# A two-layer graph network on one core: weights ahead of rows at the start, state and candidate as whole-tile operations, LeakyReLU moved to ScalarE, and new times in the planner

## The chip, the core and the metric

The kernel runs on one core of a Trainium2 chip. The core's engines each work through their own instructions in order and wait for each other by semaphores: TensorE (PE in the profile; PEld is its weight load) multiplies matrices, VectorE (DVE) does elementwise work and reductions, ScalarE (ACT) does activations and copies, GpSimd (POOL) does three tiny operations per layer norm, and SyncE (SP) issues every DMA. The metric is the device time of one execution in microseconds (us).

## The reference, cut to what matters

There are 128 graphs of 128 nodes with 256 features, all fp32. Layer 0 is a gated graph network of three steps, layer 1 is a graph attention; each has a layer norm and a ReLU in front and a residual sum behind.

```python
h = relu(layernorm(x)); A = (adj != 0)
for i in range(3):
    aggr = einsum('bst,bsd->btd', A, h @ weight[i])
    gi, gh = aggr @ w_ih.T + b_ih, h @ w_hh.T + b_hh      # split in r, z, n
    r, z = sigmoid(i_r + h_r), sigmoid(i_z + h_z)
    n = tanh(i_n + r * h_n)
    h = (1 - z) * n + z * h
x = x + h
h = relu(layernorm(x)); Wh = h @ W.T
e = leaky_relu(s1[:, :, None] + s2[:, None, :], 0.2)       # s1 = Wh @ a1, s2 = Wh @ a2
att = softmax(where(adj == 0, -inf, e))
x = x + einsum('bij,bjo->bio', att, Wh)
```

## The kernel before, in words

**Tiling.** Four graphs form a group (`G = 4`, 32 groups `g`), so a tile of features is 128 partitions by 1024 elements: two chunks of 128 features by 512 node columns. A *step* is one layer `l` of one group, 96 in all. `plan` puts them in order so that consecutive steps belong to different groups: in the middle of the run three other steps lie between two layers of one group. The last three are (31,1), (30,2), (31,2).

**One step.** `gru_step` computes the gate products with a seven-product scheme on half tiles. It runs two blocks (`blocks`), the first for reset gate and hidden candidate, the second for update gate and input candidate. Each block has seven products of mostly three matmuls each, in this order: `u` (L703), `m7` (L706), `u` again (L709), `c1[0]` (L712), `u` again (L714), `c2` (L721), `c1[1]` (L723). The bank `u` accumulates over its three products and is read between them: ScalarE copies it (L705), VectorE adds `m` to it into `c2` (L711), ScalarE copies it again (L716), VectorE adds again into `c22` (L720). TensorE can't write the third product into `u` before L711 has read it; the `c1[0]` product lies between.

Behind the products, `candidate` (L629) forms `(r+1)*v` in two operations, one for each feature half `o`. `add_half` (L780) adds the input part, `update` (L773) makes z. `state` is one task for each half: a tanh by ScalarE (L637), then three VectorE operations on 128x512 (L639, L641, L645). The second half's task to finish starts what follows: the next layer's inputs, or `epilogue`.

**Prologue and epilogue.** `prologue` normalizes a group's rows, makes the mask `A`, and transposes the rows to columns, by TensorE and ScalarE for the groups below 4 (`to_columns`, L462, L472), through DRAM by DMA for the others (`to_columns_by_blocks`). `epilogue` does the residual, the second norm and the attention. Its rows `x1` are loaded a second time (`load_x1`, L816) and added to `h` at L886; scores are formed at L903, spread by a DMA or, for the last three groups (`late`), by a TensorE transpose (L913). ScalarE adds the row score (L939, function Identity), VectorE takes `max(0.2 e, e)` (L946), masks (L952) and reduces (L958); ScalarE takes the exp (L962), `pp` is the transposed exp (L971, copied by L975), `pq` and `po` are the two products of the attention, `hs` the copy between them (L995), L1010 the final sum, then the store. The last group runs its epilogue in two parts of two graphs.

**What sets the order.** The order of every queue is written out by a planner at build time (`Order`), and the chip keeps it. Tasks yield (engine, length, time ready, room), and the planner keeps a clock for each engine: an operation starts at the later of its engine's clock and its input plus `HOP = 0.2`. `rooms` tells it when a shared buffer comes free; `fill` places elementwise work beside a product, `matmuls` places free TensorE work, `finish` runs what a step needs. The lengths are constants in the code, for example 0.62 for a 128x512 VectorE operation and `LAND = 2.5` for a DMA to land; the second load of the rows is taken as 4.0 (`LAND + 1.5`). The tile pools add the real semaphores afterwards: a wrong time in the planner gives a wait on the chip, not a wrong result.

**The start.** L92 to L133 issue the first loads from SyncE: the rows of group 0 in two DMAs, `weight[0]`, the reset part of `w_ih`, the adjacency, `w_hh` for the reset gate, the rest of `w_ih`, the rest of `w_hh`, the other weights, biases, the next groups. `given_weights` (L356) multiplies `weight[l]` into `w_ih` on TensorE, and `stationary_sums` (L321 to L339) form the weight sums of the seven-product scheme. Lines 1092 to 1099 and 1083 give the planner the times at which these are expected.

Of the kernel before, what the change touches and what calls it, by code (L numbers as in the profile page):

```python
# [14 lines left out]
P = 128  # L15
D = 256
# [11 lines left out]
def preln_gnn_kernel(  # L28
# [63 lines left out]
    xt_0 = io.tile([P, G, D], F32, tag="xt", name="xt_0", bufs=XT)  # L92
    for i in range(0, G, 2):
        dma(xt_0[:, i : i + 2, :], x[i : i + 2].rearrange("b t d -> t b d"))
    xts, ats = {0: (xt_0, (2.7, 3.7))}, {}
# [18 lines left out]
    ats[0] = load_adjacency(0), 6.4  # L114
    load_gates(whh, w_hh_t, slice(0, 1))
    load_gates(wih, w_ih_t, slice(1, 3))
# [54 lines left out]
    class Order:  # L171
        def __init__(self):
            self.free = dict.fromkeys((PE, ACT, DVE, POOL, SP, "port"), 0.0)
            self.tasks = []

            self.rooms = {"misc": [0.0] * 3, "tq": [0.0] * 2, "h": [0.0] * ROWS, "x1": [0.0] * 2, "prT": [0.0] * 2}
            self.next, self.room_of = dict.fromkeys(self.rooms, 0), {}
# [22 lines left out]
        def open(self, room, name):  # L200
# [6 lines left out]
            if room == "prT":  # L207
                return work.tile([P, G, P], F32, tag="prT", name=name)
# [220 lines left out]
    def norm_apply(src, graphs, rstd, nb, ready, name, h=None):  # L429

        for k in graphs:
            t = yield (ACT, 0.5, ready, "h") if h is None else (ACT, 0.5, ready)
            if h is None:
                h = order.open("h", f"h_{name}")
# [189 lines left out]

    def candidate(s, r, v, ready):

        for o in (1, 0):
            s.v_ready[o] = yield DVE2, 0.62, ready[o]
            put(nc.vector.scalar_tensor_tensor(  # L629
                v[:, o, :], r[:, o, :], 1.0, v[:, o, :], ALU.add, ALU.mult  # L630
            ))

    def state(s, o, old, new, v, z, ready):
# [4 lines left out]
        t = yield DVE2, 0.62, t  # L638
        put(nc.vector.tensor_tensor(new[:, o, :], old[:, o, :], n, ALU.subtract))  # L639
        t = yield DVE2, 0.62, t - HOP  # L640
        put(nc.vector.scalar_tensor_tensor(  # L641
            new[:, o, :], z[:, o, :], 1.0, new[:, o, :], ALU.add, ALU.mult
        ))
        t = yield DVE2, 0.62, t - HOP
        put(nc.vector.scalar_tensor_tensor(new[:, o, :], new[:, o, :], 0.5, n, ALU.mult, ALU.add))  # L645
        s.halves.append(t)
        if len(s.halves) == C:
            s.hT, s.aT = new, None
# [13 lines left out]
    def gru_step(s, last):  # L662
# [97 lines left out]
        s.v_ready = [0.0, 0.0]  # L760
        half_task = order.add(0, candidate(s, r, v, (banks["c1_1"], t1)))
# [395 lines left out]
```

## Time and profile before

| | |
|---|---|
| median of 3 runs | 2144.81 us (2143.91 to 2145.84) |
| the profiled execution, its own time | 2144.55 us |
| its span, first to last instruction | 2142.7 us |
| TensorE busy, matmuls | 2118.7 us (99%), 10779 records |
| VectorE busy | 1782.2 us (83%) |
| ScalarE busy | 1295.0 us (60%) |
| GpSimd busy | 119.1 us (6%) |
| mean granted TensorE clock | 0.997 |

A row of a timeline gives the start and the length in us, the engine, the line of the kernel, the operation and its tiles, and in brackets how long the engine sat idle before it and what ended that. A row of the waits names who waited for whom, the sum in us, the number of times, and the longest. A row of the groups gives the shape, the count, the busy time and the mean of one in ns. An fp32 matmul of the program leaves two records. A window's row gives the busy time of PE, PEld, DVE, ACT and POOL with the number of instructions, then the granted clock, the DMA share and the GB/s.

### The profile page before, as it was taken

The numbers are of one execution on the slowest core, as the hardware profiler recorded it, in microseconds if no ns is written. First come the engines' busy times: TensorE is split into PE (matmuls) and PEld (weight loads), VectorE is DVE, ScalarE is ACT, GpSimd is POOL, SyncE is SP. The second block draws the span as 40 slices with busy tenths as digits, with TensorE's granted clock in tenths as the row PEclk, the third lists the DMA queues.
The fourth block names the chain that finished last, engine by engine and source line by source line (L and its number), as shares of the span: only waits on it lengthen the run. The fifth ranks groups of instructions, "written<-read, shape, count | busy, mean of one in ns | idle before, by whom it ended". The sixth has DMA issues, their size and how long they took to land.

```text
span 2142.7 us, 32496 instructions
## 1 busy us (share of the span) xinstructions
PE 2118.7 (99%) x10779; PEld 1882.7 (88%) x10779; DVE 1782.2 (83%) x4176; ACT 1295.0 (60%) x2859; POOL 119.1 (6%) x204
## 2 busy tenths in 40 slices
PE   8999999999999999999999999999999999999997
PEld 7888888888888888888888888888888888888886
DVE  7778888888888888888888888888888888888776
ACT  5556656565566666656655565656656566565664
POOL 1000000000000000000000000000000000000000
PEclk9999999999999999999999999999999999999998
DMA  4144353535454255553535545354542544443301
GB/s 138 39 90 89 75 122 84 124 68 130 109 117 115 59 125 109 119 113 73 125 84 127 120 88 124 70 127 105 119 113 64 120 109 109 95 90 82 84 25 40
DMA packets 659240, 209.85 MB, mean 98 GB/s; under 512 B 569856, under 2 KB 636160, under 8 KB 659072
## 3 DMA queue, kind: packets, MB, share of 16 engines
q1 hardware_dynamic: 659072, 207.77, 43.3%
q8 instruction: 85, 1.39, 0.3%
q14 instruction: 83, 0.68, 0.1%
HBM read 120.86 MB, written 86.83 MB: 97 GB/s over the span
## 4 chain that ended last, share of the span: by engine, by line
PE 97%; DVE 2%; DMA 1%; issue 0%; SPq 0%; ACT 0%; DVEq 0%
PE c L685 34%; PE u L685 34%; PE m L685 11%; PE pa L593 8%; PE po L1003 5%; PE pq L593 3%; PE pw L356 1%; DMA x<-in_x 0%; PE pt_a L462 0%; DMA wih<-in_w_ih_t 0%; DVE prT L903 0%; DVE hT L639 0%; DMA out<-x 0%; DVE hT L641 0%; DVE c L711 0%
## 5 line engine op out<-in xcount | busy, mean ns | idle before, releaser
L773 ACT ACTIVATE z<-c,brz 128x256 f32<-128x256 f32 x384 | 185.1, 482 | 303.5 <-PE c L685 139.2
L685 PE MATMUL u<-t_h,s_hh 128*128 128x256 f32 x1152 | 343.0, 379 | 3.8 <-DVE c L711 3.8
L685 PE MATMUL c<-aT,s_f 128*128 128x256 f32 x1152 | 311.3, 379 | 0.0
L685 PE MATMUL u<-t_a,s_f 128*128 128x256 f32 x1152 | 311.3, 379 | 0.0
L738 ACT ACTIVATE r<-c,brz 128x256 f32<-128x256 f32 x384 | 174.3, 477 | 218.3 <-PE c L685 113.8
L780 DVE TENSOR_TENSOR v<-v,c 128x256 f32<-128x256 f32 x384 | 155.1, 418 | 132.1 <-ACT z L773 72.3
L685 PEld LDWEIGHTS u<-t_h,s_hh 128*128 128x128 f32 x1152 | 218.1, 190 | 34.7 <-DVE c L711 5.0
L685 PEld LDWEIGHTS u<-t_a,s_f 128*128 128x128 f32 x1152 | 218.9, 190 | 29.8
L685 PEld LDWEIGHTS c<-aT,s_f 128*128 128x128 f32 x1152 | 218.9, 190 | 29.8
L685 PE MATMUL c<-hT,s_hh 128*128 128x256 f32 x768 | 228.5, 379 | 0.0
L716 ACT COPY c<-u 128x512 f32<-128x512 f32 x192 | 109.5, 570 | 143.2 <-PE u L685 142.5
L711 DVE TENSOR_TENSOR c<-u,m 128x512 f32<-128x512 f32 x192 | 134.2, 699 | 72.4 <-PE u L685 70.4
L708 ACT COPY m<-m 128x512 f32<-128x512 f32 x192 | 112.6, 586 | 101.7 <-PE m L685 99.3
L745 ACT ACTIVATE v<-c,bhn 128x256 f32<-128x256 f32 x384 | 173.1, 481 | 0.0
L720 DVE TENSOR_TENSOR c<-u,m 128x512 f32<-128x512 f32 x192 | 131.5, 685 | 49.2 <-ACT c L716 49.2
L685 PE MATMUL m<-t_h,s_hh 128*128 128x256 f32 x576 | 171.5, 379 | 0.0
L685 PE MATMUL c<-t_h,s_hh 128*128 128x256 f32 x576 | 171.3, 379 | 0.0
L685 PEld LDWEIGHTS c<-hT,s_hh 128*128 128x128 f32 x768 | 144.8, 190 | 19.1
L685 PE MATMUL c<-t_a,s_f 128*128 128x256 f32 x576 | 155.7, 379 | 0.0
L685 PE MATMUL m<-t_a,s_f 128*128 128x256 f32 x576 | 155.6, 379 | 0.0
L685 PE MATMUL u<-aT,s_f 128*128 128x256 f32 x576 | 155.6, 379 | 0.0
L629 DVE SCALAR_TENSOR_TENSOR v<-r,v 128x512 f32<-128x512 f32 x192 | 123.4, 684 | 30.3 <-ACT v L745 28.8
(126 smaller groups left out, 3971.5 us busy)
## 6 DMA issues: line engine op xcount, KB each, us to landing
z<-tq SPq DMA_DIRECT2D x248, 128.0 KB
h<-z SPq DMA_DIRECT2D x248, 128.0 KB
xt<-in_x SPq DMA_DIRECT2D x31, 512.0 KB
z_b<-tq_b SPq DMA_DIRECT2D x116, 128.0 KB
h_b<-z_b SPq DMA_DIRECT2D x116, 128.0 KB
x<-in_x SPq DMA_DIRECT2D x29, 512.0 KB
out<-x SPq DMA_DIRECT2D x29, 512.0 KB
z_a<-tq_a SPq DMA_DIRECT2D x112, 128.0 KB
```

Source lines behind the costliest of these rows:

```text
L593: put(nc.tensor.matmul(pa[:, k * P : (k + 1) * P], h[:, k, c * P : (c + 1) * P], A[:, k, :], start=True, stop=True,))
L629: put(nc.vector.scalar_tensor_tensor(v[:, o, :], r[:, o, :], 1.0, v[:, o, :], ALU.add, ALU.mult))
L685: put(nc.tensor.matmul(to(q), S[0][:, gate_no, weight, :], moving, start=first and q == 0 and i == 0, stop=(i == len(ends) - 1), skip_grou ...
L708: put(nc.scalar.copy(m, m7))
L711: put(nc.vector.tensor_tensor(c2, u, m, ALU.add))
L716: put(nc.scalar.copy(c1[1], u))
L720: put(nc.vector.tensor_tensor(c22, u, m, ALU.add))
L738: put(nc.scalar.activation(r[:, o, cols], src, AF.Tanh, bias=brz[:, o : o + 1], scale=0.5))
L745: put(nc.scalar.activation(v[:, o, cols], src, AF.Identity, bias=bhn[:, o : o + 1], scale=0.5))
L773: put(nc.scalar.activation(z[:, o, cols], src, AF.Tanh, bias=brz[:, C + o : C + o + 1], scale=0.5))
L780: put(nc.vector.tensor_tensor(v[:, o, cols], v[:, o, cols], src, ALU.add))
L1003: put(nc.tensor.matmul(po[:, j, :], hs[:, c, k * P : (k + 1) * P], gwt[:, c, :], start=(c == 0), stop=(c == C - 1),))
```

## The change

Five things change. (1) At the start `weight[0]` and the reset part of `w_ih` are issued ahead of the rows of group 0, and the rest of `w_ih` ahead of the adjacency and of `w_hh`; the planner's times for these follow. (2) `candidate` is one operation on 128x1024 in place of two on 128x512; `state` keeps its two tanh operations, and its three VectorE operations are done once on 128x1024, after both. (3) L946 goes; the ScalarE pass at L939 uses Prelu with alpha 0.2 in place of Identity. (4) The planner takes 5.0 for the second load of the rows (4.0 before), 4.5 for the store that frees their buffer (2.5 before), and keeps rooms for `e` and `hs`. (5) Groups 2 and 3 are transposed through DRAM too. For the last two groups `e`, `hs` and the normalized rows get other buffers, one each for both parts of the last group.

```diff
-    xt_0 = io.tile([P, G, D], F32, tag="xt", name="xt_0", bufs=XT)
-    for i in range(0, G, 2):
-        dma(xt_0[:, i : i + 2, :], x[i : i + 2].rearrange("b t d -> t b d"))
-    xts, ats = {0: (xt_0, (2.7, 3.7))}, {}
...
     load_weight(0, gate, [P, 2, H], "m")
     load_gates(wih, w_ih_t, slice(0, 1))
-    ats[0] = load_adjacency(0), 6.4
+    xt_0 = io.tile([P, G, D], F32, tag="xt", name="xt_0", bufs=XT)
+    for i in range(0, G, 2):
+        dma(xt_0[:, i : i + 2, :], x[i : i + 2].rearrange("b t d -> t b d"))
+    xts, ats = {0: (xt_0, (4.8, 5.8))}, {}
+    load_gates(wih, w_ih_t, slice(1, 3))
+    ats[0] = load_adjacency(0), 8.6
     load_gates(whh, w_hh_t, slice(0, 1))
-    load_gates(wih, w_ih_t, slice(1, 3))
...
-            self.rooms = {"misc": [0.0] * 3, "tq": [0.0] * 2, "h": [0.0] * ROWS, "x1": [0.0] * 2, "prT": [0.0] * 2}
+            self.rooms = {room: [0.0] * 2 for room in ("tq", "x1", "prT", "e", "hs")}
+            self.rooms |= {"misc": [0.0] * 3, "h": [0.0] * ROWS}
...
     def candidate(s, r, v, ready):
-        for o in (1, 0):
-            s.v_ready[o] = yield DVE2, 0.62, ready[o]
-            put(nc.vector.scalar_tensor_tensor(
-                v[:, o, :], r[:, o, :], 1.0, v[:, o, :], ALU.add, ALU.mult
-            ))
+        t = s.v_ready = yield DVE2, 1.22, ready
+        put(nc.vector.scalar_tensor_tensor(flat(v), flat(r), 1.0, flat(v), ALU.add, ALU.mult))
...
         put(nc.scalar.activation(n, n, AF.Tanh, bias=bih[:, 2 * C + o : 2 * C + o + 1], scale=1.0))
-        t = yield DVE2, 0.62, t
-        put(nc.vector.tensor_tensor(new[:, o, :], old[:, o, :], n, ALU.subtract))
-        t = yield DVE2, 0.62, t - HOP
-        put(nc.vector.scalar_tensor_tensor(
-            new[:, o, :], z[:, o, :], 1.0, new[:, o, :], ALU.add, ALU.mult
-        ))
-        t = yield DVE2, 0.62, t - HOP
-        put(nc.vector.scalar_tensor_tensor(new[:, o, :], new[:, o, :], 0.5, n, ALU.mult, ALU.add))
         s.halves.append(t)
         if len(s.halves) == C:
+            n, new_, z_ = flat(v), flat(new), flat(z)
+            t = yield DVE2, 1.22, max(s.halves)
+            put(nc.vector.tensor_tensor(new_, flat(old), n, ALU.subtract))
+            t = yield DVE2, 1.22, t - HOP
+            put(nc.vector.scalar_tensor_tensor(new_, z_, 1.0, new_, ALU.add, ALU.mult))
+            t = yield DVE2, 1.22, t - HOP
+            put(nc.vector.scalar_tensor_tensor(new_, new_, 0.5, n, ALU.mult, ALU.add))
...
-        s.x1_ready = LAND + 1.5 + (yield SP, 0.45, 0.0, "x1")
+        s.x1_ready = 5.0 + (yield SP, 0.45, 0.0, "x1")
...
-        transposed = to_columns if g < 4 else to_columns_by_blocks
+        transposed = to_columns if g < 2 else to_columns_by_blocks
...
+    def place_of_e(g):
+        if g < NG - 2:
+            return order.open("e", f"e_{g}")
+        return work.tile([P, 4, H], F32, tag="th", name=f"e_{g}")[:, 0:2, :].rearrange(
+            "p n t -> p (n t)"
+        ).rearrange("p (k s) -> p k s", s=P)
...
             put(nc.scalar.activation(
-                e[:, k, :], src, AF.Identity, bias=one[:, k : k + 1], scale=1.0
+                e[:, k, :], src, AF.Prelu, bias=one[:, k : k + 1], scale=1.0, alpha=ALPHA
             ))
...
-        t = yield DVE2, row_t, t
-        put(nc.vector.scalar_tensor_tensor(le, le, ALPHA, le, ALU.mult, ALU.max))
...
-            order.close(f"x1_{g}", t + LAND)
+            order.close(f"x1_{g}", t + 4.5)
...
-    order.take(PE, 2.8, 2.2)
+    order.take(PE, 1.5, 1.0)
...
-        order.add(1, given_weights(0, wf_0, [(reset, 5.4)])),
-        order.add(1, given_weights(0, wf_0, [(others, 9.2)])),
+        order.add(1, given_weights(0, wf_0, [(reset, 4.4)])),
+        order.add(1, given_weights(0, wf_0, [(others, 8.0)])),
...
-        order.add(1, hidden_weights(((0, 7.3), (2, 10.1), (1, 11.1)))), order.add(2, biases(17.0))
+        order.add(1, hidden_weights(((0, 9.2), (2, 10.4), (1, 11.2)))), order.add(2, biases(17.0))
```

The lines of the profile before are those of the kernel before. In the changed kernel the numbers shift by 1 to 31 (L711 becomes L716, L886 becomes L903, L939 becomes L958).

## The prediction

> **What bounds the kernel now.** I read the page first, then the waits of TensorE, then the timelines of the three places where it stands idle. The page's head:
>
> ```profile
> span 2142.7 us, 32496 instructions
> PE 2118.7 (99%) x10779; PEld 1882.7 (88%) x10779; DVE 1782.2 (83%) x4176; ACT 1295.0 (60%) x2859; POOL 119.1 (6%) x204
> PE 97%; DVE 2%; DMA 1%; issue 0%; SPq 0%; ACT 0%; DVEq 0%
> ```
>
> TensorE is busy for 99% of the span and makes 97% of the chain that ended last. Work taken from VectorE is worth something only where TensorE waits. All its waits:
>
> ```profile
> PE ps L913 <- DVE prT L903: 5.6, 1, 5.6
> PE pw L356 <- DMA wih<-in_w_ih_t: 3.9, 1, 3.9
> PE u L685 <- DVE c L711: 3.8, 3, 2.5
> PE pq L593 <- ACT prT L975: 3.3, 3, 2.2
> PE po L1003 <- DVE xt L1010: 1.5, 1, 1.5
> ```
>
> The second is the start, the third lies in the middle (0.3 at 23.7 us, 2.5 near 1820, 1.0 near 1870), the others lie in the tail. The timeline at the 2.5 us wait and at the two ends:
>
> ```profile
> 6.55 3.75 PE L356 MATMUL pw<-wih,wt 128*128 128x256 f32 x8 [3.91 <-DMA wih<-in_w_ih_t]
> 32.46 1.04 PE L462 MATMUL pt_a<-ident,h_a 128*128 128x128 f32 x8
> 1812.42 1.26 SPq L60 DMA_DIRECT2D x<-in_x  x1
> 1817.31 1.29 DVE L886 TENSOR_TENSOR x<-x,h_b 128x512 f32<-128x512 f32 x2 [2.81 <-DMA x<-in_x]
> 1821.17 0.69 DVE L711 TENSOR_TENSOR c<-u,m 128x512 f32<-128x512 f32 x1
> 2107.46 0.69 DVE L645 SCALAR_TENSOR_TENSOR hT<-hT,v 128x512 f32<-128x512 f32 x1
> 2117.61 0.69 DVE L946 SCALAR_TENSOR_TENSOR e<-e 128x512 f32<-128x512 f32 x1
> 2119.76 1.09 ACT L435 ACTIVATE h_b<-xt,norm_b 128x256 f32<-128x256 f32 x2 [2.35 <-POOL norm_b L426]
> 2122.96 0.58 ACT L975 COPY prT<-pp 128x512 f32<-128x512 f32 x1 [0.31 <-PE pp L971]
> 2134.93 0.37 ACT L975 COPY prT<-pp 128x256 f32<-128x256 f32 x1 [2.66 <-PE pp L971]
> 2138.58 0.88 DVE L1010 SCALAR_TENSOR_TENSOR xt<-po,soft,xt 128x256 f32<-128x256 f32 x2 [2.72 <-PE po L1003]
> ```
>
> In the middle rows VectorE sits 2.81 us before L886, whose rows the planner took as landed. Everything behind it, L711 too, is late, and TensorE with it. The last recurrence matmul ends at 2103.61; call that T. The tail from T to the end of the span is 39.1 us, a chain over VectorE, ScalarE and TensorE.
>
> The sum is made against the profiled execution, 2144.55 us: the span and 1.85 around it. It stands 0.26 below the median of the runs.
>
> **The start: -1.3.** The reset part of `w_ih` moves from places four and five to places two and three of SyncE's queue; the two DMAs of rows move behind it, the rest of `w_ih` (two DMAs) ahead of the adjacency and two of `w_hh`. SyncE's slots are 0.5 us apart (0.72, 1.22, 1.72). The first rows, issued at 0.72, had landed by 3.49, so 2.77 is the quickest landing here; the last DMA of the reset part, issued at 2.70, landed at 6.41, so 3.71 with a megabyte ahead of it. Issued at 1.72, it lands between 4.49 and 5.43, and TensorE starts 1.0 to 1.9 earlier than at 6.55. I take 1.3, below the middle, because the rows follow at once and share the engines. The rows land up to 2 us later. In the new order TensorE does all four weight products of layer 0 (1.7 more than before) ahead of the first transposes, and this hides them: rows landed at 6.4 at the latest, plus 3.8 from there to the end of the second half's norm as before (4.78 to 8.57), plus 1 behind the copy that now stands first in ScalarE's queue, is 11.4, when TensorE is still in those products. Without this cover the rows would cost up to 1 us. The adjacency is three slots later (1.5 us); the mask is needed only by `pa`, after the transposes.
>
> **TensorE's work: -1.7, and -0.4 moved.** Two groups lose eight transposes each. The eight at 32.46 push the next product to 33.33: 0.87 a group, 1.73. The last four `pp` transposes of group 29 stood before T and now stand after it: 0.43 out of T into the tail. The two groups add 8 stores and 8 loads of 128 KB to SyncE and four VectorE transposes of 0.69; both lie under steps 2 and 3 places off (21.9 us a step), which cover a round trip of some 10 us. Without that cover the step would wait for it.
>
> **The waits at 1820 and 1870: -3.5, and +0.5 for what is late next.** The load issued at 1812.42 had its rows at 1817.31, 4.9 later; the one at 1860.05 at 1864.29, 4.2 later; the planner took 4.0 and now takes 5.0. The store ahead of the second had been issued at 1856.34, 3.7 before the load could go; 2.5 becomes 4.5. Both waits (2.5 and 1.0) should go. What is pushed back is the epilogue, which nothing on TensorE's path waits for. Next in line is L711 late for another reason: between nothing and the 3.8 of before, I take 0.5.
>
> **State and candidate as whole tiles: nothing in the middle.** The groups by shape:
>
> ```profile
> L780 DVE TENSOR_TENSOR v<-v,c 128x256 f32<-128x256 f32 x384 | 155.1, 418 | 132.1 <-ACT z L773 72.3 <-PE c L685 56.1
> L641 DVE SCALAR_TENSOR_TENSOR hT<-z,hT 128x512 f32<-128x512 f32 x192 | 132.0, 688 | 3.4
> L946 DVE SCALAR_TENSOR_TENSOR e<-e 128x512 f32<-128x512 f32 x31 | 20.6, 665 | 0.0
> ```
>
> From 418 to 688 ns is 270 for 256 columns, so 128x1024 costs about 1.22, against 1.37 for two halves: 0.15 saved, four times in 96 steps, 58 us of VectorE. L946 saves 21.5 more. VectorE falls from 1782 to about 1705 us, all of it under TensorE. The new wait is on both tanhs: the new state is ready up to 1.5 us later than with halves. Behind the waiting operation stand the epilogue's operations and the next L711. Three steps of 21.9 us lie between two layers of a group, so nobody on TensorE's path waits; at the last step there is no such cover, which the tail counts.
>
> **Prelu for Identity: nothing by itself.** The pass was there already (402 ns for 128x128 in 116 of them); both programs load one activation table. The trace has no Prelu: bounds are 0 and, for a pass as dear as the exp at L962 with its read (397 + 191 ns), 0.2 each, 24 us of a ScalarE that is 60% busy. I take 0, since the nearest row has the same shape and operands. The Trainium skill, page "ScalarE: Activation LUTs", section "Rules for kernel authors", speaks against it: relu and max belong on VectorE, not ScalarE. By that rule keeping L946 would be right, and the sum would get back its 0.7 and the 0.43 of the last group's halves in the tail; but here ScalarE reads the tile in any case, and VectorE is the fuller engine.
>
> **The tail: -5.1.** I follow the new order of the queues with the durations of these rows. T+0.4 last `add_half`; both tanhs now stand behind the last z, T+0.9 to T+2.2; meanwhile VectorE does four of group 30's score operations (1.8), which before stood behind the state. Three operations of 1.25: state at T+6.0 (before 2108.16, T+4.55), 1.45 worse. ScalarE's exps of group 29 come behind the tanhs, to T+3.75; `pp`, copy and `pq` (1.78) end at T+6.4, transposes of the state at T+6.8. VectorE has the other scores at T+8.1, the residual 0.7, the norm's statistics 1.3, POOL 1.56: first h_b at T+11.65. The mask and reduction of group 30 now stand before the second half of group 31's norm, and end at T+12.7; before, at 2120.09, T+16.5. Its exps, `pp` and copy follow at T+15.1 (before 2122.96, T+19.35). The second norm of group 31 starts its h_b at T+19.0 to 19.8 (POOL took 1.56 and 2.36 in the two cases shown) and ends at X = T+20.1 to 20.9. From there VectorE has 7.5 us of scores, sums, mask and reductions with one exp pair and the transposes: last `prT` copy at X+5.55. Before, 7.77 lay between that copy (2134.93) and the end. The span ends at T+33.4 to T+34.2; I take 34.0, 5.1 less than 39.1. Bounds: 33 (nothing else waits) and 39 (the clock, below).
>
> **Sum.** 1.3 + 1.7 + 0.4 + 3.5 - 0.5 + 5.1 = 11.5, so 2133.0 for the profiled execution and 2133.3 against the median.
>
> **Rivals.** *A cold tail, 2136.3.* The granted clock of TensorE fell to half in the half microsecond of this row:
>
> ```profile
> 2114.40 0.60 PE L913 MATMUL ps<-ident,s 128*128 128x128 f32 x4
> ...
> 2117.50:2118.00 0.50, 0.00 (x0) 0.00 (x0) 0.45 (x2) 0.00 (x0) 0.29 (x1) 0.63 0.52 186
> ```
>
> That is 2.6 us after the last matmul had ended, and the next `pq` took 3.78 for 1.78; a gap of 2.16 at T did nothing. The new order has gaps of some 2.6 (T to the first `pp`) and 2.1. By the row the first is a toss-up; a cold `pq` and `po` cost 1 to 4, I take 3. The skill's page "TensorE: Matmul & The Clock Gate", section "Why this matters for your kernels", puts the limit at gaps of about 3 us: by it the tail stays warm, and the sum is unchanged.
>
> *The loads stay late, 2136.8.* If the landing spreads beyond 5.0, the waits of 3.5 stay or move. 4.9 is close to 5.0; but 56 of the 58 L886 had no such wait even with 4.0.
>
> *A whole-tile operation in front of L711, the other side.* TensorE's `c1[0]` product lasts 1.29 and L711 with its hops 0.7, so L711 may be 0.6 late. VectorE keeps order: a 1.22 operation begun a little late holds it. In the new order 40 of the 192 L711 have such an operation directly ahead. Above about 19 lost waits of 0.6 (11.5 us) the change is no gain; all 40 would give 2157. Against it: 84 of 192 have a 0.69 operation directly ahead now, and none but the three shown lost anything; row durations summed over the VectorE instructions between L720 and the next L711 leave at least 1.2 us in every block, as before.
>
> *The rows at the start are late, 2135.* The cover above fails and 1 to 2 come back.
>
> **How the numbers follow.** Likeliest 0.45 (2131 to 2136); cold tail 0.22; loads 0.12; whole-tile stalls 0.13, of which some 0.08 beyond the gain; start 0.08. The range 2130.5 to 2142 takes in the first three, the start and the milder stalls. The three runs spread over 0.09%, so 0.2% (4.3 us) tells a change from none. Faster, below 2140.5: 0.85; within 0.2%: 0.05; slower: 0.10.
>
> **What would show it.** Right: the first `pw` near 5.3; no wait of PE for L716 (L711's new place) near any L903 (L886's) with a DMA behind it; 5428 program matmuls; the new L647 to L651 near 1.22; one table load; T near 2097; first `pp` of the tail at half or full clock settles the cold rival. Wrong: many PE waits on L716 behind L636 or L647 to L651, or a tail of 39.

## The result and the profile after

The changed kernel takes 2141.05 us, median of 7 runs (2135.69 to 2142.27), where the kernel before, run beside it, takes 2144.81 (2143.91 to 2145.84). The ratio is 0.9976, 95% interval 0.9966 to 0.9985: it is faster, but by 3.8 us where 11.5 were forecast. Its profiled execution took 2138.47 us, 2.6 less than the median, and most of what follows is about that spread.

The head of its page, then TensorE's waits (who waited for whom, the sum in us, how often, the longest):

```profile
span 2136.7 us, 32121 instructions
...
PE 2119.0 (99%) x10763; PEld 1879.0 (88%) x10763; DVE 1724.6 (81%) x3763; ACT 1302.4 (61%) x2855; POOL 105.9 (5%) x204
...
PE 96%; DMA 1%; ACT 1%; DVE 1%; SPq 1%; issue 0%; POOL 0%; DVEq 0%; ACTq 0%; POOLq 0%
```

```profile
PE pp L988 <- ACT e L979: 4.3, 3, 2.7
PE pq L598 <- DMA e<-z_e: 3.0, 4, 1.8
PE pq L598 <- ACT prT L992: 2.3, 4, 0.7
PE pw L357 <- DMA wih<-in_w_ih_t: 1.6, 2, 1.2
...
PE u L690 <- DVE c L716: 0.3, 1, 0.3
```

What was to go went: the wait for the first weights is 1.6 instead of 3.9, and of the 3.8 on L711 (now L716) only the 0.3 of the start is left. New is the second row. It lies in the middle of the run: the product `pq` of the attention waits for `e`, which comes back transposed through DRAM (stores `z_e<-prT`, loads `e<-z_e`). The first and third rows belong to the tail.

To see the middle and the tail apart I use two numbers for every run. T is the end of the last recurrence matmul, the tail is the span behind it. The *time lost before T* is T minus TensorE's work up to there, taken from the order of its instructions at the spacing of undisturbed rows (0.431 us for 256 columns, 0.2225 for 128, 0.108 for a transpose). It holds the start, every wait, and slow matmuls. "Low clock" is the length of the tail, in half microseconds while matmuls were still to come, in which the granted clock was below full. Each ratio is to the kernel before as timed beside that run.

| run | median us (runs) | ratio to before, 95% | T | lost before T | tail | low clock in the tail |
|---|---|---|---|---|---|---|
| before | 2144.81 (7) | | 2103.60 | 15.7 | 39.1 | 10.5 |
| after | 2141.05 (7) | 0.9976 (0.9966 to 0.9985) | 2101.29 | 15.6 | 35.4 | 4 |
| e5, after again | 2140.65 (10) | 0.9975 (0.9966 to 0.9985) | 2104.84 | 19.1 | 35.5 | 4 |
| e13, after again | 2142.02 (11) | 0.9982 (0.9973 to 0.9991) | 2104.88 | 19.2 | 38.8 | 7 and 7.5 |
| e17, after again | 2142.22 (10) | 0.9982 (0.9973 to 0.9991) | 2105.84 | 20.1 | 35.3 | 4 |
| e1, ten idle products | 2139.71 (5) | 0.9968 (0.9955 to 0.9981) | 2103.66 | 17.9 | 35.5 | 4 |
| e2, planner: `e` later | 2166.70 (4) | 1.0094 (1.0079 to 1.0109) | 2126.68 | 41.0 | 38.0 | 7 and 3.5 |
| e3, halves | 2139.00 (5) | 0.9963 (0.9950 to 0.9976) | 2102.75 | 11.4 | 34.7 | 17.5 |
| e4, before + two times | 2140.66 (10) | 0.9976 (0.9966 to 0.9986) | 2098.42 | 10.5 | 39.7 | 4 and 7 |
| e6, `e` by POOL | 2148.74 (10) | 1.0011 (1.0002 to 1.0021) | 2108.12 | 22.4 | 36.2 | 7.5 |
| e7, before + start | 2144.82 (10) | 0.9999 (0.9990 to 1.0008) | 2103.26 | 15.4 | 39.3 | 4 and 7.5 |
| e8, halves, filled | 2140.54 (10) | 0.9971 (0.9962 to 0.9980) | 2105.67 | 12.5 | 34.0 | 4 and 4 |
| e9, rows by POOL | 2136.97 (5) | 0.9962 (0.9949 to 0.9975) | 2099.21 | 13.5 | 36.0 | 7.5 |
| e10, whole tiles, order of e3 | 2193.70 (4) | 1.0222 (1.0207 to 1.0237) | 2157.58 | 66.2 | 34.5 | 7.5 and 7.5 |
| e11, before + Prelu | 2145.11 (10) | 0.9997 (0.9988 to 1.0007) | 2104.56 | 16.7 | 38.6 | 11 |
| e12, e10 filled | 2194.49 (4) | 1.0224 (1.0207 to 1.0241) | 2158.11 | 66.7 | 34.6 | 14.5 |
| e14, e9 again | 2136.99 (5) | 0.9962 (0.9949 to 0.9974) | 2098.27 | 12.5 | 37.5 | 7 and 4 |
| e15, e9, first gap filled | 2136.55 (4) | 0.9960 (0.9946 to 0.9973) | 2098.23 | 12.5 | 36.7 | 7.5 |
| e16, e9, both gaps filled | 2134.35 (5) | 0.9948 (0.9935 to 0.9962) | 2098.15 | 12.4 | 34.4 | 0 |

T fell by 2.3 in the first profile. 2.16 of it is work taken out or moved behind T, as counted in the forecast. The time lost before T is the same as before although the start gained 1.8 and the old waits of 3.5 are gone: some 5 us came in somewhere. Here is the longest place, from the timeline of the changed kernel (start, length, engine, line, operation, tiles, and in brackets the idle time before; only the rows that bear on it, and of the four stores `z<-tq` the last three):

```profile
371.87 2.69 SPq L60 DMA_DIRECT2D z<-tq  x3
...
376.65 0.70 DVE L571 STREAM_TRANSPOSE prT<-e 128x512 f32<-128x512 f32 x1
378.14 3.12 SPq L60 DMA_DIRECT2D h<-z  x4
381.31 2.79 SPq L60 DMA_DIRECT2D z_e<-prT  x4
384.16 0.61 SPq L60 DMA_DIRECT2D x<-in_x  x1
385.78 1.71 SPq L60 DMA_DIRECT2D e<-z_e  x4
389.66 2.02 PE L598 MATMUL pq<-e,h_b 128*128 128x128 f32 x16 [1.81 <-DMA e<-z_e]
```

VectorE has `prT` ready at 377.35. The stores of `z_e` could go then, but in SyncE's order the loads `h<-z` of another group stand in front of them, and these wait until their own stores (the last issued by 374.56) have landed, at 378.14: 3.6 us, where the planner's `LAND` is 2.5. So the stores of `z_e` begin 3.96 us late, the loads of `e` end 10.1 us after the transpose, and `pq`, which the order puts 10.34 us behind the transpose, waits 1.81. Followed back, the chain that ended last in this stretch goes from `pq` over the landings of `e` and `z_e` to SyncE's issuing of `h<-z` at 378.

In the kernel before, the stores of `z_e` began 0.02 to 0.08 us after the transpose in all 24 groups up to 1800 us. In the new order every third group has `h<-z` in between: in the eight from 377 to 1747 us the stores began 1.4 to 4.0 us late, while in the other two of three they start at 0.02 to 0.04. That is where two runs of one program part: the first profile and e5 keep their distance within 0.1 us for some 200 us at a time, and it changes at such a `pq` (by 0.2 at 388 us, 0.4 at 585, 0.8 at 781, -0.5 at 975, -0.2 at 1367, 0.8 at 1563, 0.7 at 1758). One more change, 0.8, lies at 1824, where L716 waits 0.7 in e5. How long each trip takes varies; the place hardly does.

### The profile page after: what moved, and what is told of

The parts are those of the page before. It is cut to its first block, busy times and chain, and to the rows that moved or that the text cites. A ratio compares the mean times of both kernels' runs of the same rounds, so it can differ in the third digit from the quotient of the medians.

```text
span 2136.7 us, 32121 instructions
## 1 busy us (share of the span) xinstructions
PE 2119.0 (99%) x10763; PEld 1879.0 (88%) x10763; DVE 1724.6 (81%) x3763; ACT 1302.4 (61%) x2855; POOL 105.9 (5%) x204
## 4 chain that ended last, share of the span: by engine, by line
PE 96%; DMA 1%; ACT 1%; DVE 1%; SPq 1%; issue 0%; POOL 0%; DVEq 0%; ACTq 0%; POOLq 0%
PE c L690 34%; PE u L690 34%; PE m L690 11%; PE pa L598 8%; PE po L1027 5%; PE pq L598 3%; PE pw L357 1%; SPq L60 1%; DMA e<-z_e 1%; DMA z_e<-prT 0%; ACT e L979 0%; DMA wih<-in_w_ih_t 0%; ACT v L642 0%; PE pr_o L489 0%; DVE v L785 0%
## 5 line engine op out<-in xcount | busy, mean ns | idle before, releaser
L716 DVE TENSOR_TENSOR c<-u,m 128x512 f32<-128x512 f32 x192 | 134.0, 698 | 144.9 <-PE u L690 144.7
L721 ACT COPY c<-u 128x512 f32<-128x512 f32 x192 | 109.4, 570 | 117.3 <-PE u L690 116.9
L725 DVE TENSOR_TENSOR c<-u,m 128x512 f32<-128x512 f32 x192 | 132.0, 687 | 37.5 <-ACT c L721 36.0
L710 ACT COPY c<-u 128x512 f32<-128x512 f32 x192 | 109.5, 570 | 53.3 <-PE u L690 53.3
```

What stands on the lines that cost most here:

```text
L710: put(nc.scalar.copy(c1[0], u))
L716: put(nc.vector.tensor_tensor(c2, u, m, ALU.add))
L721: put(nc.scalar.copy(c1[1], u))
L725: put(nc.vector.tensor_tensor(c22, u, m, ALU.add))
```

## Experiments

Where a kernel has products of the identity by itself on TensorE (called idle products below), they only keep it busy, and nobody reads their result.

**e1: ten idle products in front of each `pp` of the tail.**

```diff
+            if g < NG - 1:
+                for _ in range(10):
+                    put(nc.tensor.matmul(m7[:, 0, 0:P], ident, ident, start=True, stop=True))
             for k in graphs:
                 put(nc.tensor.transpose(pp[...], e[:, k, :], ident))
```

> Changed kernel, plus ten 128x128 matmuls of the identity into the idle bank m7 in front of the transposed exps (pp) of groups 29 and 30, where TensorE has nothing to do; the order of all else is kept, and no output changes. Theory A (the spread of 2135.7 to 2142.3 of the changed kernel is a cold TensorE clock in the tail): no window of the tail is below full clock, the first pq of the tail takes about 1.8 in place of 3.6, the tail from the last recurrence matmul to the end is about 34 in place of 35.4, the runs agree within 2 us and the median falls to 2135 to 2137. Rival B (the spread comes from DMA waits in the middle): spread and median stay, 2138 to 2142.

The times lie closer (2137.88 to 2140.94), but the tail is 35.5, as in after. The clock fell all the same, at T+5.5, though no idle stretch of TensorE there was longer than 0.7 us: ahead of it TensorE had been busy for 2.2 of 3.5 us. So one long gap isn't what it takes. T came 2.4 later than in after with the same order up to there: the middle varies from run to run.

**e2: the planner is told that `e` lands 2.5 us later.**

```diff
-        return (yield from by_way_of_dram(
+        return 2.5 + (yield from by_way_of_dram(
```

> Changed kernel; the planner is told that the transposed attention e lands 2.5 us later than it took, and nothing else. Theory A (TensorE waits in the middle because pq is placed before e can have come back through DRAM): the waits of PE on e<-z_e, 5.1 us on TensorE's weight loads in the changed kernel, fall below 1, and the last recurrence matmul ends near 2096 to 2097 in place of 2101.3; median 2136 to 2138. Rival B (the whole-tile operations or the queue as a whole are late, so that waits only move): the sum of PE's waits between 50 us and the tail stays 3 or more, the time 2140 to 2142.

A miss, and an instructive one. The new time made another order, in which `pq` still waits and more waits come in:

```profile
PE u L690 <- DVE c L716: 15.1, 9, 2.8
...
PE pq L598 <- DMA e<-z_e: 3.9, 4, 1.9
```

Their cause is the same kind of trip: in this order VectorE stands in front of L458 for the features that come transposed through DRAM (`hT_a<-z_a`, 19.7 us in 9 waits, 3.5 at most), and L716 behind it is late. Here one corrected time put another trip where it is short; e4 below shows that it can also go well. The waits cost more than their own length: behind five of them (1.9 to 2.8 us each) the granted clock stood at 0.50 for 3.41 us in the middle of the run, first at 388.92, which happened in no other trace before T.

**e3: after, planned and written with state and candidate in halves as before.**

```diff
-        t = yield DVE2, 1.22, max(s.halves)
-        put(nc.vector.tensor_tensor(new_, flat(old), n, ALU.subtract))
+        t = yield DVE2, 0.62, t
+        put(nc.vector.tensor_tensor(new[:, o, :], old[:, o, :], n, ALU.subtract))
 ...
```

> Changed kernel with candidate and state on halves of 128x512 as before; start, Prelu, planner times and transposes stay as changed. Theory A (the waits on e<-z_e come from the planner's DMA times): 2 to 6 us of DMA waits of PE stay, time within 3 us of the changed kernel (2138 to 2144). Rival B (the whole-tile operations make e late): no PE wait on e<-z_e, last recurrence matmul near 2096.5. In the tail the state is ready near T+4.6 in place of T+6.0.

```profile
PE pr_o L489 <- DVE hT L653: 6.0, 1, 6.0
PE pp L991 <- ACT e L982: 4.0, 1, 4.0
...
PE pa L598 <- DMA h<-z: 0.6, 1, 0.6
```

No wait on `e` is left, and 11.4 us are lost before T. Here, up to 1940 us, `pq` stands 11.63 us behind the transpose in every group, and the stores of `z_e` begin 1.0 to 2.6 us after it, so the trip fits. Planning with the whole-tile times thus brought in the order that is short in every third group.

**e4: before, with only the two times for the second load of the rows.**

```diff
-        s.x1_ready = LAND + 1.5 + (yield SP, 0.45, 0.0, "x1")
+        s.x1_ready = 5.0 + (yield SP, 0.45, 0.0, "x1")
...
-            order.close(f"x1_{g}", t + LAND)
+            order.close(f"x1_{g}", t + 4.5)
```

> Kernel before, with only the planner's two times changed: 5.0 for the second load of the rows, 4.5 for the store that frees their buffer. Theory A (those two times remove the waits on L711 behind L886 and bring others only by chance): no wait of PE on L711 in the middle (3.5 before), time 2141 if nothing takes their place. Rival B (longer times push the epilogue into SyncE's queue and make other DMAs late, as in the changed kernel): PE waits on e<-z_e of 2 or more appear, time 2142 to 2146.

The waits at 1820 and 1870 are gone (0.3 on L711 is left, at the start) and nothing came in their place: by its progress against the profile of before it gains 2.8 near 1820 us and 1.3 more near 1870. These two constants alone make a kernel as fast as the whole change (0.9976 for both). Up to 1750 us it already lies 1.18 ahead, with a start that isn't changed at all; see the last section.

**e7: before, with only the new start.**

```diff
     load_gates(wih, w_ih_t, slice(0, 1))
-    ats[0] = load_adjacency(0), 6.4
+    xt_0 = io.tile([P, G, D], F32, tag="xt", name="xt_0", bufs=XT)
+    ...
+    load_gates(wih, w_ih_t, slice(1, 3))
+    ats[0] = load_adjacency(0), 8.6
...
-    order.take(PE, 2.8, 2.2)
+    order.take(PE, 1.5, 1.0)
```

> The kernel before with only the new order of the first loads and the planner's start times. My sum of the start said 1.3 us; the profile of the changed kernel shows 1.8. If it is 1.8 by itself, T falls from 2103.6 to about 2101.8, or as far as 2100.5 if the start runs at the full clock throughout, the waits at 1820 and 1870 stay within 1 us of 3.5 and the time is 1 to 2.5 us below the kernel before. Rival: the rows that now land later hold the first transposes, and the time is that of the kernel before within 0.5.

From 400 to 1750 us it runs 1.24 ahead of the profile of before, near the 1.3 of the forecast; but e4, with the old start, ran 1.18 ahead, so this profile alone shows nothing (see the last sections). Then the waits at 1820 and 1870 take 4.5 instead of 3.5. In the times (0.9999) it can't be told from before.

**e5: the changed kernel once more.** No edit.

> The changed kernel once more, unaltered, profiled on another occasion. If the waits in the middle belong to the written order, the waits of TensorE on e<-z_e stand at the same places with the same sizes (1.8 near 388 us, 5.1 in all in the weight loads' row), lost time before T is 15.6 as before, and the time is 2141 within 1 us. If they depend on how long each transfer through DRAM happens to take, the sum moves by 1 to 3 us between the two profiles (lost time before T 13 to 18) and the tail stays at 35.4 within 0.5.

T is 3.55 later with the same order, by the steps told above; the tail is 35.5. The waits on `e` are 5.0 in 7.

**e6: the trip of `e` issued by POOL.**

```diff
-            G, t, f"{name}_e",
+            G, t, f"{name}_e", queue=nc.gpsimd,
```

> The changed kernel with the order of PE, DVE and ACT untouched; only the eight transfers that bring the attention tile e through DRAM are issued by POOL instead of SyncE. Theory A (SyncE issues in order, and the trip of e stands behind transfers that are held for another tile's landing): the waits of TensorE on e<-z_e fall from 5.1 to under 1, lost time before T from 15.6 to 11 or 12, the time by about 4 us to 2136 or 2137. Theory B (the trip itself is too long for its place in the order, whoever issues it): the waits stay above half of 5.1 and the time stays at 2140 to 2142. A cost that could spoil it: POOL is held behind a landing, its norms come late, and TensorE then waits on h_b instead.

Worse: 2148.74. The stores now begin 0.3 to 0.5 us after the transpose (once 1.6), but the loads of `e` go only 6.4 to 8.2 us after it in every third group, and the waits are 6.6. For transfers that POOL issues the trace also has the landings, and they say why: in all 29 groups the loads begin 0.66 to 0.74 us after the last of the four stores has landed. In the eight groups in question, where SyncE issues `h<-z` from 0.4 us before the transpose to 1.8 us behind it, that store lands 2.9 to 4.7 us after its issue has ended, in most others 1.6. So in this run the trip is too long though nothing holds it in its queue: next to other transfers the stores land late. The hold in SyncE can't be the whole cause.

**e9: the loads that bring rows back (`h<-z`) issued by POOL instead, the trip of `e` left on SyncE.** The order of PE, DVE and ACT is that of after.

```diff
-            tmp.rearrange("p i g c f -> p (i g c) f"), place, C * G, t, name, "h"
+            tmp.rearrange("p i g c f -> p (i g c) f"), place, C * G, t, name, "h", nc.gpsimd,
```

> The changed kernel with the order of PE, DVE and ACT untouched; only the four loads that bring a tile of rows h back from DRAM (h<-z) are issued by POOL instead of SyncE, so that they hold nobody on SyncE while they wait for their stores to land. In every third group of the changed kernel the stores of z_e began 1.4 to 4.1 us after prT was transposed, and pq comes 10.34 us behind that transpose. Theory A (SyncE's order): these stores begin within 0.5 us, the loads of e within 5 us, the waits of TensorE on e<-z_e fall from 5 to under 0.5, lost time before T falls to 11 to 13, the time to 2136 to 2138. Theory C (the transfers share the 16 DMA engines, so whatever stands next to them slows them): the loads of e still go 6 us or more after the transpose, the waits stay above 3 and the time at 2140 or more. A cost that could hide A: rows that land later hold the products pa.

The same place as above, in its timeline:

```profile
376.36 0.70 DVE L571 STREAM_TRANSPOSE prT<-e 128x512 f32<-128x512 f32 x1
377.07 1.93 POOL L60 DMA_DIRECT2D h<-z  x4 [5.17 <-PE u L690]
377.09 4.01 SPq L60 DMA_DIRECT2D z_e<-prT  x4
381.20 0.57 SPq L60 DMA_DIRECT2D x<-in_x  x1
383.79 1.73 SPq L60 DMA_DIRECT2D e<-z_e  x4
387.40 1.95 PE L598 MATMUL pq<-e,h_b 128*128 128x128 f32 x16
```

The stores begin 0.03 us after the transpose, and `pq` follows at 10.34 without a wait. In all groups up to 1822 us the stores begin within 0.04. Two waits are left (2.0 in all, at 583 and 780), and the loads of `e` still go 5 to 7.3 us after the transpose where 4.3 is the quickest: the other expectation, that the transfers also slow each other, holds for a part, as in e6. The Trainium skill, page "Trainium Kernel Development and Optimization", section "Key Constraints", says that issuing from several engines saves only the sequencer's issue time, since all share the same 16 DMA engines; here it also took a held instruction out of the way, and the move was worth 5 us (e13 and e14 below). How much of that is the hold, and how much the way in which the transfers then fall beside each other, these runs don't part.

**e13 and e14: after and e9 once more, side by side.** No new edit.

> The changed kernel, timed beside e14 on the same chip. If the waits on e in the middle differ from run to run, as between its two profiles (T 3.55 apart with one order), its profile again shows a lost time before T somewhere between 15 and 20, the tail at 35.4 within 0.3, and the times spread over 4 us or more around 2141.

> e9 once more, against the changed kernel on the same chip. If SyncE's order is where most of the missing gain went, e14 is faster than e13 by 2.5 to 5 us in the median, and in the profile the stores of z_e begin within 0.1 us of the transpose in all groups up to 1800 us, with 1 to 3 us of waits on e<-z_e left. If e9's gain was the luck of its runs, the two agree within 1 us.

2142.02 against 2136.99, 5.0 us apart (intervals 0.9973 to 0.9991 and 0.9949 to 0.9974, which touch but hardly overlap). In the profiles the time lost before T is 19.2 against 12.5, 6.6 us by T, of which the waits on `e` show 4.4 (5.8 against 1.4). The starts of the two agree within 0.1 us, so the difference lies in the middle. The tail of e13 is 38.8, for 35.4 in the first profile with the same order. Its timeline:

```profile
2109.87 3.79 PE L598 MATMUL pq<-prT,h_b 128*128 128x128 f32 x16 [0.68 <-ACT prT L992]
...
2122.21 3.78 PE L598 MATMUL pq<-prT,h_b 128*128 128x128 f32 x16 [0.68 <-ACT prT L992]
...
2126.21 4.71 PE L1027 MATMUL po<-gwt,hs 128*128 128x256 f32 x16
```

Both `pq` ran at half clock; in the first profile of after only the first did (3.60, then 2.05).

**e15 and e16: e9 with the idle stretches of the tail filled,** in e15 in front of the first `pq` alone, in e16 of both.

```diff
+            fill = NG - 3 <= g < NG - 1          # e15: g == NG - 3
+            warm((10 if g == NG - 3 else 7) * fill)
             for k in graphs:
                 put(nc.tensor.transpose(pp[:, k * P : (k + 1) * P], e[:, k, :], ident))
+                warm(fill)
+            warm(2 * fill)
```

> e9 with products of the identity by itself on TensorE, read by nobody, that fill the idle stretches from T to the first pq of the tail: 10 ahead of the first pp, one behind each of its four transposes, 2 ahead of pq. It asks what the cold clock costs the tail, and whether the clock falls only where TensorE has little to do over some microseconds. If both hold, the granted clock stays at 1.0 up to that pq, which takes 1.8 instead of 3.6 us, and the tail falls from the 35.4 to 36.0 of the changed kernel and e9 to 34.0 to 34.6, near the 34.0 of my sum for a warm tail. If the clock falls all the same, or the tail stays at 35.4 or above with a warm clock, the rest of the tail's shortfall lies with VectorE and ScalarE.

> e15 with the same filling of the second idle stretch of the tail as well (7 products of the identity ahead of the second group's pp, one behind each of its transposes, 2 ahead of its pq). In e15 the first pq took 2.05 us instead of 3.6, but the clock fell at T+13.5, the second pq took 3.79 and the two po behind it 4.12, and the tail was 36.7. If the clock now stays at 1.0 over both, the second pq takes about 1.9, its po 3.6, and the tail falls by 2 to 3 us to 33.7 to 34.7, the forecast's 34.0 for a warm tail; the time by as much, to 2134 or 2135. If the tail stays at 36 or more with a warm clock, VectorE and ScalarE set it and the clock does not.

In e15 the first `pq` took 2.05, but the clock fell at T+13.5 and the second took 3.79: tail 36.7. In e16 the clock never fell. From its list of cores (span and mean clock) and its timeline:

```profile
core 0: 2132.6 us, clock 1.000
```

```profile
2102.99 2.05 PE L598 MATMUL pq<-prT,h_b 128*128 128x128 f32 x16
...
2113.77 2.05 PE L598 MATMUL pq<-prT,h_b 128*128 128x128 f32 x16
...
2115.87 3.91 PE L1035 MATMUL po<-gwt,hs 128*128 128x256 f32 x16
```

The tail is 34.4, the time 2134.35 (2133.84 to 2134.71), ratio 0.9948 (0.9935 to 0.9962). The kernel is the change with the loads `h<-z` on another queue and 29 products that nobody reads, and it is 7.9 us faster than the change itself beside it (e17). How much of that the products bring is less sure: the intervals of e9 and e16 overlap, but the tail is 1.5 to 3 us shorter.

**e17: after beside e16.** No edit.

> The changed kernel on the same chip for the comparison with e16: 2140 to 2142.5, with a tail of 35.4 where only one stretch of the tail is at the low clock and near 38.8 where two are, as in e13.

2142.22, tail 35.3 with one stretch at the low clock.

**e8: e3 with idle products in the last gaps.**

```diff
+            if g == NG - 1 and pairs[0] == 0:
+                warm(16)
             banks, ready = yield from to_rows(s.hT, ready, f"{name}_o", pairs)
...
+            if g < NG - 1:
+                warm(8)
             for k in graphs:
                 put(nc.tensor.transpose(pp[...], e[:, k, :], ident))
```

> The changed kernel with the state and the candidate in halves as before (as in e3), and on TensorE 16 products of the identity by itself ahead of the last state's transposes and 8 ahead of the first pp, which only keep TensorE busy (their results are read by nobody). In e3 the clock was at half from T+3 to T+20 and pr_o, pp, pq and po took 1.9, 1.6, 3.8 and 2.4 us, which is 4.5 more than at full clock. If the cold clock is on the path of the tail, the tail falls from 34.7 to between 30.5 and 32.5 and the time to 2135 to 2137 in e3's conditions. If the tail is bound by VectorE and ScalarE, it stays at 34 or more.

The tail fell by 0.7 where 2 to 4 were expected, though the low clock fell from 17.5 to 8 us; 8 of the products came to stand in front of T (1.8 us at 0.2225 each). In this order the gaps are long (6.0 and 4.0 in e3), which suggests that the low clock lies partly beside VectorE's chain; no run shows it.

**e10: whole-tile operations without their order.** The order of e3 on PE, ACT and SyncE, each whole-tile operation at the place of the second half.

```diff
         t = yield DVE2, 0.62, t
-        put(nc.vector.tensor_tensor(new[:, o, :], old[:, o, :], n, ALU.subtract))
+        if second(0):
+            put(nc.vector.tensor_tensor(flat(new), flat(old), flat(v), ALU.subtract))
+        else:
+            put(nc.vector.tensor_tensor(new[:, o, 0:1], old[:, o, 0:1], n[:, 0:1], ALU.subtract))
 ...
```

> The order of e3 (the changed kernel planned with halves) kept on PE, ACT and SyncE, but the state's three operations and the candidate's are issued over the whole tile, each at the place of the second half; the first half leaves one subtraction of a single column. It parts the whole-tile operations from the order that the planner makes with them. Theory: by themselves they cost nothing and take 55 to 60 us from VectorE; TensorE has no wait in the middle on the rows c or e<-z_e (under 0.7 in all besides the start), T lies within 1.2 of e3 (the start varies by that), and the time at 2138 to 2140. Rival (the whole-tile operation holds VectorE in front of L716): TensorE waits on c for 2 us or more in the middle and the time is above 2141.

The rival came true. Waits of TensorE, and one of the places in the timeline:

```profile
PE u L701 <- DVE c L736: 14.0, 54, 0.4
...
PE u L701 <- DVE c L727: 4.2, 9, 0.5
```

```profile
711.50 1.22 DVE L656 SCALAR_TENSOR_TENSOR hT<-z,hT 128x1024 f32<-128x1024 f32 x1
711.82 0.57 ACT L732 COPY c<-u 128x512 f32<-128x512 f32 x1 [0.40 <-PE u L701]
...
712.75 1.23 DVE L661 SCALAR_TENSOR_TENSOR hT<-hT,v 128x1024 f32<-128x1024 f32 x1
...
713.89 0.69 DVE L736 TENSOR_TENSOR c<-u,m 128x512 f32<-128x512 f32 x1
...
714.63 0.70 PE L701 MATMUL u<-hT,s_hh 128*128 128x256 f32 x2 [0.26 <-DVE c L736]
```

L736 (L725 of after) could start at 712.4, when ScalarE's copy ends, but two operations of 1.2 us stand ahead, and it starts at 713.89. The product between covers 1.29 of it. 63 such waits show as 18.2 us, and T is 54.8 later than in e3: the rest stands in rows that count as busy (PE 2150.0 for 2118.1). 54 of the 63 are at L736, the second of the two reads of the bank, where the rival had named the first. So the whole-tile operation costs nothing only in an order that was made with its 1.22; put into another, it costs some 0.9 a wait.

**e12: e10 with 16 idle products behind T.**

```diff
+            if g == NG - 1 and pairs[0] == 0:
+                warm(16)
             banks, ready = yield from to_rows(s.hT, ready, f"{name}_o", pairs)
```

> e10 with 16 products of the identity by itself on TensorE right behind T, ahead of the last state's transposes, which only keep TensorE busy. In e8 these and 16 others gave 0.7 off the tail and cost 1.8 ahead of T; here none stands ahead of T. Expected: T as in e10, the tail 0.5 to 1 shorter than e10's, the time 0.5 to 1 below e10's. If VectorE's and ScalarE's chain alone sets the tail, it is as long as e10's within 0.3.

The tail stayed (34.6 for 34.5): filling one gap alone did nothing here. The low clock began at T+6.9 instead of T+2.7, and there was as much of it.

**e11: before, Prelu for Identity and no L946, order kept.**

```diff
-                e[:, k, :], src, AF.Identity, bias=one[:, k : k + 1], scale=1.0
+                e[:, k, :], src, AF.Prelu, bias=one[:, k : k + 1], scale=1.0, alpha=ALPHA
...
-        put(nc.vector.scalar_tensor_tensor(le, le, ALPHA, le, ALU.mult, ALU.max))
```

> The kernel before with its order kept; Prelu takes the place of Identity, and L946, VectorE's maximum, is left out. By my sum nothing changes up to T, since VectorE only loses 20.6 us under TensorE (the L711 waits of 3.5 may move by 1), and the tail loses between 0.7 and 1.1: 2144 to 2146. If a Prelu is dearer than Identity (402 ns), by as much as 0.2, the tail of 39.1 gains nothing. Prelu's own duration settles it.

Prelu takes as long as Identity. The group of this pass in e11, 116 of 128x128 (the last number is the mean in ns; in before 402):

```profile
L939 ACT ACTIVATE e<-e,s 128x128 f32<-128x128 f32 x116 | 37.7, 403 | 0.3 <-DMA e<-line 0.3
```

The tail is 0.5 shorter, T 1.0 later (0.4 of it at the start, the rest behind 1000 us), and the time can't be told from before.

## Why the forecast was half right

**The start, -1.3: held in the mean.** It is 1.77 in the profile of after, where the third `u` product starts at 22.81 instead of 23.72 with one weight product of 0.86 more behind it. A single profile can't show it, since e4 gained 1.1 and e11 lost 0.3 with the old start. But at 30 us the sixteen profiles with the new start are 0.6 to 2.3 ahead of that of before, 1.35 ahead of the mean of the three with the old one. The rows of group 0 held nobody: the first transposes come right behind the weight products.

**TensorE's work, -1.73 and -0.43: held** by the count, 2.16 out of T.

**The waits at 1820 and 1870, -3.5: held** (0.6 or 0.7 came back at 1824 in e5, e13 and e17), and e4 shows that the two times do it alone. **"And +0.5 for what is late next": this step failed.** The forecast looked for it at L711, between nothing and 3.8, and said of the epilogue that nothing on TensorE's path waits for it. `pq` does. Between the runs of the new start without held trips (11.4 to 13.5 lost before T) and the four profiles of after (15.6, 19.1, 19.2, 20.1) lie 2 to 9 us, 6 to 7 in the pair that ran side by side. The first profile was the luckiest of the four, which fits its lying 2.6 below the median. The clue was there to be read by comparing the two orders: only in the new one does `h<-z` stand in front of `z_e<-prT` in every third group. And the forecast itself had read landings of 2.77 to 4.9 us; the planner's 2.5 was exceeded here with 3.6.

**State and candidate as whole tiles, nothing in the middle: right for the operations, wrong for their order.** They take what was worked out:

```profile
L636 DVE SCALAR_TENSOR_TENSOR v<-r,v 128x1024 f32<-128x1024 f32 x96 | 117.4, 1223 | 20.2 <-ACT v L750 18.4
L649 DVE SCALAR_TENSOR_TENSOR hT<-z,hT 128x1024 f32<-128x1024 f32 x96 | 117.0, 1219 | 0.6
```

and the 40 places where one stands directly in front of L711 cost at most 0.7 besides the start in any profile of after. The planner had placed them with their length; e10 shows the rival's mechanism, and that its price of 0.6 a wait was low. But planning with them moved the attention's trip, and no step of the forecast asked what else moves when every time in a planner shifts. VectorE's busy time fell by 57.6 us, not 77: the rows added up do fall by 75.5, but neighbouring rows of its queue overlap, and busy time counts an overlap once. As forecast, that by itself was worth nothing.

**Prelu, nothing: held**, 398 ns in after and 403 in e11 for 402.

**The tail, 39.1 to 34.0: the order was read rightly, the clock wasn't.** The state is ready at T+6.0 as worked out, and the first `pp` waits 2.7 for the 2.6 foreseen. But here are the first `pq` of the tail in the timeline of after, and its window:

```profile
2106.13 3.60 PE L598 MATMUL pq<-prT,h_b 128*128 128x128 f32 x16 [0.68 <-ACT prT L992]
```

```profile
2106.00:2108.00 2.00, 1.87 (x8) 1.87 (x9) 1.90 (x7) 0.08 (x1) 0.00 (x0) 0.50 0.00 0
```

The clock is 0.50 (the third number from the end) and `pq` takes 3.60. The state's transposes behind it come at T+8.3, in e16 at T+6.7, and the tail is 35.4 for 34.4 there: the low clock's 1.6 cost 1.0 at the end. That is the rival of the cold tail, a toss-up in the forecast; it came in every profile of this order, once with a second stretch (38.8, more than its price of 3). e16 is the test: with no low clock the tail is 34.4 for the forecast's 34.0.

So both misses have been undone by experiment: with the loads `h<-z` out of SyncE's way and the clock kept up, the kernel takes 2134.35, where 2133.3 was forecast. The other terms of the sum came out about right; missing were waits in the middle worth 2 to 9 us, for which 0.5 had been taken, and a low clock worth 1 to 4.5 in the tail, for which nothing had.

## What to carry to other kernels

When a change alters the lengths that a planner works with, compare the two orders queue by queue, SyncE's too, and look for instructions that came to stand behind one that waits; the operation that was changed is the least of it. A transfer that waits, and holds others behind it, can be given another queue without a new order; which one is moved matters (e9 gained, e6 lost). At a sparse end of a kernel, idle products that fill TensorE's short gaps can pay.

## What the runs showed of the hardware

*The low clock doesn't need a long gap.* The forecast drew the line at an idle stretch of 2.6 us. In e1 the clock fell with no gap over 0.7, and in e16, with none over 0.5 and TensorE nearly always busy, it never did. The stretches at the low clock measure 3.41, 6.83, 10.24, 13.65 and 17.07 us in the traces' clock record (after, e9, before, e12, e3), whole multiples of 3.41, and within each of the 19 traces all changes of the clock lie on one grid of that step. The Trainium skill, page "TensorE: Matmul & The Clock Gate", section "Part 1: The HAM clock gate", describes a free-running window of 3.4 us over which activity is watched; the lengths agree with it. The gap of about 3 us, which the prediction cites from that page as the limit, doesn't agree with e1. With the traces cut into these steps, full clock was followed by half after every step in which TensorE's matmul rows fill less than 1.5 us, and after none with more than 2.2; between the two both happened. Half was followed by full after every step with 2.79 or more, and after none with 2.77 or less. Tails of the one order go with the total: 34.4 at 0, 35.3 to 35.5 at 4, 36.0 to 36.7 at 7.5, 37.5 at 11, 38.8 at 14.5.

*The start varies by over 1 us for the same reason.* In before, the first transposes (eight, at 10.09) took 1.78; in e4, with the same start, 1.04 at 9.76, and it stayed 1.18 ahead. The granted clock reads 1.00 there in both, but only because a trace's clock record begins with its first rise to full, and a window ahead of that has nothing in it. That rise stands at 11.61 us in before, 9.43 in e4 and 12.48 in e11, and the rows agree: in before, the transposes take 421 ns each until 11.4 and about 272 behind e4's rise. Half of the 2.18 us between before and e4 is 1.09 of the 1.18. With the new start the rise comes between 7.7 and 12.1 us.

*A store of 128 KB and a load behind it vary.* The same held trip at 377 us began 3.96, 4.11, 3.81 and 3.19 us late in the four profiles of one order, that at 770 us 1.64, 2.25, 1.88 and 2.52, and made waits of 0.3, 1.1, 1.3 and 1.1. In e9 the wait at 780 us is 1.8 though the loads had been issued 5.4 us before `pq` ran; what held that landing is open.
